# A graph network layer on one core: block 1's positions and five derived matrices at other places of the start

## The chip, the core and the metric

The kernel runs on one core of one Trainium2 chip. The core has TensorE (PE in the profile; its weight loads are PEld), VectorE (DVE), ScalarE (ACT), GpSimd (POOL) and SyncE (SP), each with a queue of its own that it works off in program order. The metric is the device time of one execution in microseconds; lower is better.

## The reference

128 graphs of 64 nodes with 128 channels; `adj` is 0 or 1, symmetric, with about one edge in eight. For every edge a message is computed by a three-layer network from the two nodes' rows, summed at the receiving node, and a second three-layer network updates the nodes:

```python
def _mlp(x, w0, b0, g0, be0, w1, b1, g1, be1, w2, b2):
    h = relu(x @ w0 + b0)
    h = layernorm(h, g0, be0)
    h = relu(h @ w1 + b1)
    h = layernorm(h, g1, be1)
    return h @ w2 + b2

messages = _mlp(concat([f_i, f_j]), *msg) * coupling_matrix[..., None]
agg = sum(messages, axis=2)
updated = part_feats + _mlp(concat([part_feats, agg]), *upd)
```

All of it is float32. The eight message and update weights are 128x128 (the first layers 256x128).

## The kernel before, in words

**Tiles.** Only existing edges are computed. Two graphs make a pair p (64 pairs); each graph has 640 slots for its edges, five tiles of 128. A quad q is two pairs, 20 tiles, five chunks n of four tiles (512 edges), so there are 160 chunks. A block b is four pairs (16 blocks, ten chunks each).

**Edges to slots.** For a block, `rank` (VectorE, L359) scans the adjacency rows, `count` (TensorE) and `count_out` (ScalarE) give running totals, and `place` (GpSimd, L384 to L388) makes the tile `pos`, the slot of each edge. `place_out` (L397, two GpSimd instructions) multiplies it by the adjacency into `posall`, which has one half for even and one for odd blocks. For a pair, `distance` (ScalarE, L482) and `make_tp` (VectorE, L488) make a 0/1 matrix from slot to receiving node, `marks` (L513, TensorE) multiplies it with `posall`, and `compare` (L521, VectorE) gives the matrix of the sending nodes. Both are copied by DMA into the tile `s` (`stack`, L504).

**Layers.** `rows` (L453 and L455) multiplies a block half's nodes with the first layer's weights in the PSUM bank `mu`; `rows_hi` (ScalarE, L467, `abh`) and `rows_lo` (VectorE, L473, `abl`) take it out. `layer0` (L539) multiplies `s` with these rows into the one bank `hps`, and ScalarE takes it out with a relu as `h` (L542). `stats0` transposes `h` (L548) and takes the statistics (L552). `layer1` (L609) runs eight iterations behind, in the banks `z0` and `z1` in turn; its bias times each edge's standard deviation is put there first, either by ScalarE (`seed`, L597, six chunks in ten) or by a matmul (L606) with `sdT`, the turned deviations, and a table `b1t`. ScalarE takes it out as `y` (L612), `stats1` (L619) follows. `weights` (L682) and `reduce` (L695) sum over the edges of a node, and a `Unit` of each block applies the update network.

**Standard deviations.** Once per quad: `var0_of` (five small GpSimd instructions, L249 to L253), `root_of` (ScalarE `m_sd` L259, then `sh` on ScalarE L566 and GpSimd L567), `turn_root` (TensorE, L572) and `root_out` (ScalarE, `sdT`, L577).

**Derived matrices.** `derivation` makes 13 matrices of the weights once: a layer norm's gain and centring are folded into the next layer's weights (`centred`: ScalarE scales to `wg`, L177; a product with the matrix of means, L181; VectorE subtracts, L186), its shift into the next bias (`shift`: ScalarE broadcasts `beb`, L204; two products, L207 and L208; a ScalarE copy, L197), and some are products or transposes (`plain`, L212, L216, copy L197). The first eight, up to `c2u`, belong to the message network and to the link between both; the last five (`ub0b`, `u1c`, `bu1b`, `u2c`, `cu2b`) are needed by the units alone, the first of which starts at iteration 23. `bias_table` (iteration 3: ScalarE `b1hi` L647, then GpSimd L649 to L653) and `bias_part` (GpSimd, L659, iterations 4 to 8) make the table `b1t` from `b1b`.

**The order.** It is written out by hand. After a start section with the first three chunks of layer 0, a loop runs over iterations n; `at(n, place, fn, ...)` puts a piece of work into place "a", "m", "b", "k", "x", "x1", "x2", "e0", "e1" or "e" of an iteration:

```python
        for n in range(last + 1):
            run(n, "a")
            run(n, "m")
...
                layer1(n - L1)
            run(n, "b")
...
                layer0(n if n >= QC else n + LEAD)
...
                stats0(n - 1 if n > QC else n + 1)
            run(n, "k")
...
                stats1(n - L1)
            for k in ("x", "x1", "x2", "e0", "e1", "e"):
                run(n, k)
```

Here QC is 5, LEAD is 3 and L1 is 8. Iterations 0 and 1 hold chunks 3 and 4 of layer 0; iterations 2 to 4 hold none; from iteration 5 on, iteration n holds chunk n of layer 0, and from iteration 8 on, chunk n - 8 of layer 1. The queue of each engine holds its part of this order.

A derived matrix with place n has its ScalarE preparation at (n-1, "x"), its products at (n, "x") and what takes it out at (n+1, "m"). The 13 matrices have the places 1, 2, 4, 5, 6, 7, 9, 10, 11, 12, 14, 15, 16, and all use the one `mu` bank (`ubank`), as do `rows` (block 1: iterations 8 and 13) and the units. The `z` banks serve the start section's marks, and then layer 1 from iteration 8 on. For block 1, `place` is at (2, "e") and `place_out` at (4, "e"); the marks of its first pair (4) are at iterations 5 and 6. For later blocks `place_out` is seven iterations ahead of the block's first chunk.

After the loop a path for graphs that don't fit stands behind a flag and isn't taken.

Of the kernel before, what the change touches and what calls it, by code (L numbers as in the profile page):

```python
# [23 lines left out]
def tile_gnn(  # L24
# [50 lines left out]
    QC = QT // CH  # L75
# [91 lines left out]
    nball = const.tile([P, NB], F32, name="nball")  # L167
    W = {}

    def derivation(bank):  # L170


        def centred(w, g, name):

            def ahead():
                wg = W[name, "g"] = const.tile([P, C], F32, name="wg", bufs=2)
                nc.scalar.activation(wg, w, AF.Copy, scale=g)  # L177

            def product():
                ps = bank()  # L180
                nc.tensor.matmul(ps[:, :C], lhsT=mean_m, rhs=W[name, "g"], start=True, stop=True)  # L181
                return ps

            def empty(ps):
                W[name] = const.tile([P, C], F32, name=name)
                nc.vector.tensor_tensor(W[name], W.pop((name, "g")), ps[:, :C], op=ALU.subtract)  # L186
            return ahead, product, empty

        def plain(name, fn, ahead=lambda: None):
            def product():  # L190
                ps = bank()
                fn(ps[:, :C])
                return ps

            def empty(ps):
                W[name] = const.tile([P, C], F32, name=name)
                nc.scalar.copy(W[name], ps[:, :C])  # L197
            return ahead, product, empty

        def shift(w, be, bias, name):  # L200

            def ahead():
                beb = W[name, "b"] = const.tile([P, P], F32, name="beb", bufs=2)
                nc.scalar.copy(beb, be.to_broadcast([P, P]))  # L204

            def fn(ps):
                nc.tensor.matmul(ps, lhsT=W.pop((name, "b")), rhs=w, start=True, stop=False)  # L207
                nc.tensor.matmul(ps, lhsT=ones_row, rhs=bias, start=False, stop=True)  # L208
            return plain(name, fn, ahead)

        def product_of(l, r, name):
            return plain(name, lambda ps: nc.tensor.matmul(ps, lhsT=l(), rhs=r, start=True,  # L212
                                                           stop=True))

        def turned(w, name):
            return plain(name, lambda ps: nc.tensor.transpose(ps, W[w], ident))  # L216

        return [
            centred(w1, g0c, "w1c"),
            shift(w1, be0c, b1r, "b1b"),  # L220

            centred(w2, g1c, "w2c"),
            turned("w2c", "w2cT"),
            product_of(lambda: W["w2cT"], u0b, "w2u"),
            shift(w2, be1c, b2r, "c2b"),
            turned("c2b", "c2bT"),
            product_of(lambda: W["c2bT"], u0b, "c2u"),
            product_of(lambda: ones_row, ub[0], "ub0b"),
            centred(u1, ug[0], "u1c"),
            shift(u1, ube[0], ub[1], "bu1b"),  # L230
            centred(u2, ug[1], "u2c"),
            shift(u2, ube[1], ub[2], "cu2b"),
        ]
# [55 lines left out]
    def edge_path(es):  # L289
# [32 lines left out]
        def zbank(k):  # L322
            return ps_z[k].tile([P, CH * C], F32, name=f"z{k}")
# [4 lines left out]
        def at(n, place, fn, *args):  # L328
            plan.setdefault((n, place), []).append((fn, args))
# [482 lines left out]
        for b in range(NB):  # L812
            o = b * CPB
            if b > 1:
                at(max(o - 25, 0), "a", load_adj, b)
                at(max(o - 12, 0), "a", load_x, b)
            if b > 0:
                r = max(o - 12, 1)
                at(max(o - 14, 0), "m", rank, b)
                at(r, "x", count, b)  # L820
                at(r + 1, "a", count_out, b)
                at(r + 1, "a", degrees, b)
                at(max(o - 9, r + 1), "e", place, b)
                at(max(o - 7, r + 3), "e", place_out, b)
                at(max(o - 7, 13), "m", odd_weights, b)
                at(o - 3, "x", turn_x, b)
                at(o - 2, "a", turn_x_out, b)
            for half, n in ((0, o - 2), (1, o + 3)):
                if n >= 0:
                    at(n, "x2", rows, b, half)  # L830
                    at(n + 1, "a", rows_hi, b, half)
                    at(n + 1, "m", rows_lo, b, half)
        for b in reversed(range(NB)):
            o = b * CPB
            n = o + QC + SC
# [35 lines left out]
        for p in range(NP):  # L871
            n = p * TG * 2 // CH
# [18 lines left out]
        for q in range(NQ):  # L891
            n = q * QC + QC if q else LEAD
# [86 lines left out]
        def turn_x_out_rest():  # L979
            nc.scalar.copy(blocks[0]["xnT"][:, 2 * P:PB * P], blocks[0].pop("x_ps")[:, 2 * P:])  # L980

        for n, (ahead, product, empty) in zip([n for n in range(1, 20) if n % QC != 3],
                                       derivation(ubank)):
            def keep(n=n, product=product):
                W["ps", n] = product()
            at(n - 1, "x", ahead)
            at(n, "x", keep)
            at(n + 1, "m", lambda n=n, empty=empty: empty(W.pop(("ps", n))))
        at(3, "b", bias_table)
        for c in range(QC):  # L990
            at(4 + c, "e", bias_part, c)
# [55 lines left out]
    with ExitStack() as es:  # L1047
        es.enter_context(tc.manual_schedule())
        flag = edge_path(es)
# [160 lines left out]
```

## Time and profile before

| | us |
|---|---|
| median of 4 runs | 577.57 |
| lowest and highest of them | 575.86, 577.91 |
| the profiled execution | 576.62 |
| its span, first to last instruction | 574.9 |
| TensorE busy | 549.0 |
| VectorE busy | 479.5 |
| ScalarE busy | 476.8 |
| GpSimd busy | 339.4 |

Lines of the profile name the engine, the source line, the operation, and what it writes from what it reads. In a timeline the first two numbers are start and duration in us, and the bracket at the end says how long the engine stood idle before and what released it. A timeline joins neighbouring instructions of one kind. Where instructions of one engine follow each other without a gap, the step from one start to the next is what one costs; the durations overlap a little. Of a matmul the end is modelled. Windows give, for a stretch, its length and the busy time of PE, PEld, DVE, ACT and POOL (with the number of instructions), then the granted TensorE clock (1.00 is full), the DMA engines' busy share and GB/s.

### The profile page before, as it was taken

How to read it: one execution, taken by the hardware profiler on the slowest of the kernel's cores; microseconds unless marked ns; L12 is line 12 of the kernel's file. 1: busy time of each engine (PE TensorE's matmuls, PEld its weight loads, DVE VectorE, ACT ScalarE, POOL GpSimd, SP SyncE). 2: the span in 40 equal slices, each digit the busy share in tenths (PEclk: the TensorE clock that was granted, in tenths of full speed). 3: DMA queues.
4: the chain of work that ended last, by engine and by line, in shares of the span. 5: the costliest groups of instructions: out<-in, count | busy, mean ns of one | idle time of the engine just before them, and what ended most of it. 6: DMA issues, size and time to landing. Idle time of an engine off the chain costs nothing. (4 is left out here: it accounts for less than half of the span.)

```text
span 574.9 us, 15748 instructions
## 1 busy us (share of the span) xinstructions
PE 549.0 (95%) x5303; PEld 514.9 (90%) x5303; DVE 479.5 (83%) x1944; ACT 476.8 (83%) x1149; POOL 339.4 (59%) x898
## 2 busy tenths in 40 slices
PE   6798999999999999999999999999999999998894
PEld 4587889999999999999999999999999999988883
DVE  5668789797989889798989979798988979896686
ACT  6677979898888989898888989888898989886434
POOL 3344465665757666565767656575766656556342
PEclk8889999999999999999999999999999999999998
DMA  4464536465554555468553654555376564631201
GB/s 101 102 144 106 130 94 141 94 115 130 125 133 106 140 110 130 105 110 153 111 143 83 139 115 116 127 125 133 93 144 116 123 107 100 135 93 33 34 21 40
DMA packets 90769, 63.21 MB, mean 110 GB/s; under 512 B 57398, under 2 KB 74812, under 8 KB 90684
## 3 DMA queue, kind: packets, MB, share of 16 engines
q1 hardware_dynamic: 90396, 62.03, 49.1%
q8 instruction: 43, 0.70, 0.5%
q14 instruction: 42, 0.34, 0.2%
q10 hardware_dynamic: 288, 0.13, 0.1%
HBM read 6.82 MB, written 4.19 MB: 19 GB/s over the span
## 5 line engine op out<-in xcount | busy, mean ns | idle before, releaser
L552 DVE BATCH_NORM_STATS2 st<-hT 128x6 f32<-128x128 f32 x640 | 141.9, 284 | 36.7 <-PE hT L548 35.2
L609 PE MATMUL z<-w1c,h 128*128 128x128 f32 x1280 | 172.2, 277 | 0.0
L609 PEld LDWEIGHTS z<-w1c,h 128*128 128x128 f32 x1280 | 161.0, 192 | 8.3 <-issue 5.1
L597 ACT ACTIVATE z<-b1b,m_sd 128x128 f32<-128x128 f32 x360 | 133.6, 371 | 8.7
L619 DVE BATCH_NORM_STATS2 st<-y 128x6 f32<-128x128 f32 x640 | 137.5, 276 | 2.7 <-ACT y L612 1.4
L612 ACT ACTIVATE y<-z 128x512 f32<-128x512 f32 x160 | 94.5, 591 | 26.7 <-PE z L609 24.9
L542 ACT ACTIVATE h<-hps,b0c 128x512 f32<-128x512 f32 x160 | 109.4, 684 | 3.8 <-PE hps L539 3.7
L548 PE MATMUL hT<-ident,h 128*128 128x128 f32 x640 | 98.2, 276 | 1.6 <-DVE st L552 1.5
L682 POOL TENSOR_TENSOR w<-oh,m_q 128x320 f32<-128x320 f16 x126 | 91.9, 741 | 9.9 <-PE hT L548 5.3
L539 PE MATMUL hps<-s,abl 128*128 128x512 f32 (+3 forms) x256 | 93.4, 376 | 1.7 <-DVE abl L473 0.9
L548 PEld LDWEIGHTS hT<-ident,h 128*128 128x128 f32 x640 | 76.8, 142 | 11.9 <-ACT h L542 1.3
L497 POOL CAST i<-tp 128x640 fp32r<-128x640 f16 x58 | 41.6, 717 | 66.7 <-DVE tp L488 48.7
L539 PE MATMUL hps<-s,abh 128*128 128x512 f32 (+3 forms) x256 | 79.5, 329 | 0.0
L695 PE MATMUL ys<-y,w 128*64 128x128 f32 x1280 | 76.9, 275 | 0.0
L695 PEld LDWEIGHTS ys<-y,w 128*64 128x64 f32 x1280 | 69.2, 137 | 4.2 <-issue 3.6
L249 POOL TENSOR_TENSOR m_d<-st 128x20 f32<-128x20 f32 x62 | 16.3, 263 | 91.0 <-DVE st L552 78.0
L521 DVE TENSOR_TENSOR j<-mk,cmpt 128x320 fp32r<-128x320 f32 x124 | 58.6, 472 | 3.1 <-PE mk L513 3.1
L539 PEld LDWEIGHTS hps<-s,abl 128*128 128x128 f32 x256 | 50.2, 196 | 3.6 <-ACT h L542 2.1
L482 ACT ACTIVATE d<-slot,mid 128x640 f16<-128x640 f16 x64 | 52.7, 824 | 0.0
L539 PEld LDWEIGHTS hps<-s,abh 128*128 128x128 f32 x256 | 50.5, 197 | 0.0
L473 DVE TENSOR_TENSOR abl<-mu,abh 128x512 fp32r<-128x512 f32 (+1 forms) x33 | 22.3, 675 | 31.3 <-ACT abh L467 31.1
L513 PE MATMUL mk<-tp,posall 128*128 128x320 f16 x126 | 38.3, 304 | 3.5 <-POOL posall L397 2.5
(224 smaller groups left out, 977.3 us busy)
## 6 DMA issues: line engine op xcount, KB each, us to landing
s<-i SPq DMA_DIRECT2D x124, 160.0 KB, 2.7
s<-j SPq DMA_DIRECT2D x124, 160.0 KB, 2.6
xn<-in_x_dram SPq DMA_DIRECT2D x15, 256.0 KB, 3.8
out_dram<-uo SPq DMA_DIRECT2D x15, 256.0 KB, 2.4
an<-in_adj_dram SPq DMA_DIRECT2D x16, 128.0 KB, 2.7
oh<-tp SPq DMA_TRANSPOSE x64, 3.4
xn<-in_x_dram SPq DMA_DIRECT2D x2, 128.0 KB
out_dram<-uo SPq DMA_DIRECT2D x2, 128.0 KB, 2.6
```

The lines of the kernel that those rows point to most:

```text
L482: nc.scalar.activation(D[p], slot, AF.Abs, bias=blocks[b]["mid"][:, q:q + 1], scale=-1.0)
L521: nc.vector.tensor_tensor(JR[p][:, c], MK.pop((p, k))[:, 0:HC], cmpt[:, c], op=ALU.is_equal)
L539: nc.tensor.matmul(ps[:, c:c + w], lhsT=ab[:, g % 4, :], rhs=s, start=(k == 0), stop=(k == 1))
L542: nc.scalar.activation(H[n], ps, AF.Relu, bias=b0c)
L548: nc.tensor.transpose(ps[:, t, :], H[n][:, t * P:(t + 1) * P], ident)
L552: nc.vector.bn_stats(ST0[q][:, CH * c + t, :], ps[:, t, :])
L597: nc.scalar.activation(Z[n][:, t, :], W["b1b"], AF.Copy, scale=SR[q][:, k:k + 1])
L609: nc.tensor.matmul(ps[:, t, :], lhsT=h[:, t * P:(t + 1) * P], rhs=W["w1c"], start=False, stop=True, skip_group_check=True)
L612: nc.scalar.activation(Y[n], ps, AF.Relu)
L619: nc.vector.bn_stats(ST1[q][:, CH * c + t, :], Y[n][:, t, :])
L682: (nc.vector if p == NP - 2 else nc.gpsimd).tensor_tensor(WT[p][:, :, g, :], OH[p][:, :, g * N:(g + 1) * N], Q[q][:, k:k + TG].unsqueeze(2 ...
L695: nc.tensor.matmul(YS[b][g * N:(g + 1) * N, k, :], lhsT=w[:, t, g, :], rhs=y, start=(t == 0), stop=(t == TG - 1))
```

## The change

Two things are moved; no operation is added or removed. `place_out` of block 1 goes from (4, "e") to (3, "a"). The last five derived matrices go from the places 11, 12, 14, 15 and 16 to 2, 3, 4, 5 and 6, and use the banks `z0` and `z1` (place n takes `z` of n % 2) instead of `mu`. At one place the steps of the first eight come first. `product` is now given its bank.

```diff
-    def derivation(bank):
+    def derivation():
...
-            def product():
-                ps = bank()
+            def product(ps):
                 nc.tensor.matmul(ps[:, :C], lhsT=mean_m, rhs=W[name, "g"], start=True, stop=True)
-                return ps
...
-                at(max(o - 7, r + 3), "e", place_out, b)
+                at(*((r + 2, "a") if b == 1 else (o - 7, "e")), place_out, b)
...
-        for n, (ahead, product, empty) in zip([n for n in range(1, 20) if n % QC != 3],
-                                       derivation(ubank)):
-            def keep(n=n, product=product):
-                W["ps", n] = product()
+        steps = derivation()
+        for n, k, bank in ([(n, k, ubank) for k, n in enumerate((1, 2, 4, 5, 6, 7, 9, 10))] +
+                           [(n, 6 + n, lambda n=n: zbank(n % 2)) for n in range(2, 7)]):
+            ahead, product, empty = steps[k]
+
+            def keep(n=n, k=k, bank=bank, product=product):
+                W["ps", k] = bank()
+                product(W["ps", k])
             at(n - 1, "x", ahead)
             at(n, "x", keep)
-            at(n + 1, "m", lambda n=n, empty=empty: empty(W.pop(("ps", n))))
+            at(n + 1, "m", lambda k=k, empty=empty: empty(W.pop(("ps", k))))
```

For block 1, r is 1 and o is 10; for b above 1, `o - 7` is what the maximum gave before.

More of the change, by code (lines that the diff above doesn't have):

```diff
@@ L189, in plain, with product @@
         def plain(name, fn, ahead=lambda: None):
-            def product():
-                ps = bank()
+            def product(ps):
                 fn(ps[:, :C])
-                return ps
             def empty(ps):
```

## The prediction

> **What bounds the kernel now.** I read the page first, then the waits of TensorE between 20 and 70 us, then the engines' timelines there, then windows cut where the granted clock changes.
>
> ```profile
> span 574.9 us, 15748 instructions
> PE 549.0 (95%) x5303; PEld 514.9 (90%) x5303; DVE 479.5 (83%) x1944; ACT 476.8 (83%) x1149; POOL 339.4 (59%) x898
> ...
> PEclk8889999999999999999999999999999999999998
> ```
>
> TensorE (PE) is the bound: busy 95%. What the change touches lies in the first 65 us, where PE has gaps. Its waits there (us in total, times, longest):
>
> ```profile
> PE mk L513 <- POOL posall L397: 2.5, 1, 2.5
> PE ma L572 <- POOL sh L567: 2.0, 2, 1.2
> PE mu L181 <- DVE abl L473: 1.4, 1, 1.4
> PE mu L453 <- DVE u1c L186: 1.3, 1, 1.3
> ```
>
> The first and the last have to do with the change: block 1's positions late by 2.5 us, and the u1c subtraction holding the one mu bank for 1.3 us ahead of `rows`. But a wait that goes is worth only the distance to the next one. For the first I read ScalarE's (ACT) timeline:
>
> ```profile
> 22.38 0.27 ACT L197 COPY b1b<-mu 128x128 f32<-128x128 f32 x1 [0.47 <-PE mu L208]
> 22.68 0.30 ACT L647 CAST b1hi<-b1b 128x128 fp32r<-128x128 f32 x1
> ...
> 26.73 0.31 ACT L259 ACTIVATE m_sd<-m,eps_c 128x20 f32<-128x20 f32 x1 [1.79 <-POOL m L253]
> 27.07 0.22 ACT L566 CAST sh<-m_sd 128x40 fp32r<-128x40 f32 x1
> 27.20 0.72 ACT L495 CAST i<-tp 128x640 fp32r<-128x640 f16 x1
> 27.82 0.82 ACT L482 ACTIVATE d<-slot,mid 128x640 f16<-128x640 f16 x1
> 28.56 0.67 ACT L542 ACTIVATE h<-hps,b0c 128x512 f32<-128x512 f32 x1
> ```
>
> The last row empties the only hps bank, and ends at 29.23. PE's next layer 0 (chunk 6) needs that bank and started at 29.47. So nearly all of the 2.5 us wait lies beside a second one: ACT works in program order, and this eviction stands behind a root that waits for GpSimd (POOL), which ran `bias_table` and `var0_of(0)` from 23.06 to 26.70, started by b1hi.
>
> **GpSimd's part.** `place_out(1)` moves from behind the `sh` subtraction (27.59, 1.52 us) to iteration 3's start. POOL ends `pos` at 21.61 and was idle until b1lo at 23.06, so the 1.52 us fit into 1.45 us of hole; b1lo would be 0.07 late, less than the 0.30 below. It is moved past no DMA. If the marks of pair 3 (22.98) had to wait for the same tile, they lose about 0.15 us, which the ACT chain covers; bounds 0 and 0.15, I take 0. Behind it, `bias_part` ends some 1.3 us earlier than at 34.68; no one waits for it.
>
> **What the five steps add to iterations 2 to 7.** Slots (start to start) from the same operations later in the trace: ub0b 0.41 on PE, bu1b and cu2b 0.32 + 0.41 = 0.73 each (55.81 to 56.54), u1c and u2c 0.14 each (48.95 to 49.09): 2.15 us. ACT: three copies of about 0.20, two weight scalings of 0.29, two broadcasts of 0.19: 1.56 us. VectorE: two subtractions of 0.20. Their vectors were issued by 12.3 us, ahead of need at 21; the z banks are free until iteration 8. No DMA is added.
>
> On PE, ub0b, u1c and bu1b push layer 0 of chunk 5 from 25.96 to about 26.95 and the marks of pair 4 to 27.65. That is hidden: both end before the ACT eviction. The cost is on ACT. The ub0b copy stands between b1b and b1hi: its product ends at about 22.75, so b1hi starts at 22.98, 0.30 late, and POOL's chain and m_sd with it. Behind m_sd come the u2 scaling (0.29) and the bu1b copy (0.20), ahead of the eviction: 28.56 + 0.30 + 0.29 + 0.20 = 29.35. It ends at 30.02, so chunk 6's layer 0 starts at 30.05 instead of 29.47, 0.58 late.
>
> From there PE is solid until layer 1 of chunk 0 (34.75 before), and its clock decides:
>
> ```profile
> 5.32:8.73 3.41, 1.77 (x19) 1.02 (x18) 2.85 (x6) 2.81 (x6) 2.67 (x7) 1.00 0.46 111
> ...
> 12.14:15.56 3.42, 2.56 (x9) 1.75 (x9) 1.74 (x5) 2.65 (x5) 0.00 (x0) 0.50 0.21 39
> ...
> 22.38:25.80 3.42, 1.90 (x22) 1.43 (x22) 2.55 (x9) 1.45 (x4) 2.56 (x7) 1.00 0.80 199
> 25.80:29.21 3.41, 0.91 (x5) 0.48 (x6) 0.45 (x2) 2.45 (x5) 2.40 (x7) 1.00 0.60 141
> 29.21:32.62 3.41, 3.41 (x15) 3.14 (x16) 2.98 (x8) 1.94 (x6) 3.41 (x3) 0.50 0.36 87
> ```
>
> The second column is PE's busy time, the third from the end the granted clock. It changes on a grid of 3.41 us. A stretch with PE busy 0.91 us (27%) was followed by a closed clock (0.50), one with 1.77 (52%) too; one with 1.90 (56%) was not. In the closed stretch chunk 6's layer 0 to chunk 7's took 29.47 to 32.30 = 2.83 us; at full clock the same slots are 0.67 (43.78 to 44.45) + 0.44 (44.45 to 44.89) + 0.14 (marks) + 0.15 (62.43 to 62.58) + 0.14 (42.52 to 42.66) = 1.54. So closed time loses 1 - 1.54/2.83 = 46%, 1.56 us per stretch.
>
> In the changed kernel PE has work from 26.05 to about 28.1, 2.05 us or 60% of the stretch 25.80 to 29.21 on this grid: it keeps the clock, narrowly. Then layer 0 of chunk 7 starts at 30.05 + 1.54 + 0.73 (cu2b) = 32.32, against 32.30, and takes 0.56 (47.81 to 48.37) where it took 0.71: **fill -0.1 us**. With one closed stretch it is -0.1 + 1.56 = +1.5.
>
> The Trainium skill ("TensorE: Matmul & The Clock Gate", "HAM oscillation") gives the rule as no PE gaps above about 3.4 us; the trace differs, since a gap of 2.5 us sufficed. By that rule the clock would hold here whatever the order, and only the -0.1 would stand; the row decides. The same page (Part 1) calls the window free-running and not reset at a kernel's start: then the grid falls elsewhere in each run. One trace can't show that; it speaks against counting on the clock.
>
> **What leaves iterations 11 to 17.** ub0b: the next matmul needs sdT, which ACT ended at 46.64, and started at 46.66: 0.06, not 0.41. u1c: 0.14.
>
> ```profile
> 52.89 0.32 PE L453 MATMUL mu<-w0a,xnT 128*64 128x128 f32 x1 [1.31 <-DVE u1c L186]
> ```
>
> Without the subtraction `rows` starts 1.3 + 0.2 us earlier. But ACT is solid from 48.09 to 54.72; only the 0.19 broadcast and the 0.06 go there, so abh starts at 53.90 and the y eviction of chunk 6 at 54.38 (55.10 before), the h eviction of chunk 14 ends at 55.55, and layer 0 of chunk 15, which needs its bank, runs at 55.6 (57.46): 1.86. VectorE, solid as well, starts the statistics of chunk 14 at 57.25 (58.64): 1.39. POOL, root and `turn_root(2)` follow: 61.04 (62.43). Next on PE, cu2b's 0.73 is gone: layer 1 of chunk 9 at 61.19 (63.30), 2.11. ACT, behind the root, reaches y of chunk 9 at 62.67 (64.50): 1.83. Both engines are nearly solid from there, and both must be earlier for the rest: bounds 1.39 (the root chain) and 2.11 (PE); I take **1.85**, ACT's, which is last.
>
> **Sum.** -1.85 - 0.1 = -1.95 us. The profiled execution took 576.62 around its span of 574.9; that gives 574.67. It lies 0.95 below the median of 577.57, inside the runs' 575.86 to 577.91, so I carry the difference to the median: 575.6.
>
> **Rivals.** (B) The clock closes once in the fill: -1.85 + 1.5 = -0.4, 577.2. For it: 60% is near the 56% and 52% on either side, and on a grid shifted by 1 us (26.8 to 30.2) PE's work is only 1.45 us, 43%. Against: the grid of this trace; and a shifted grid can also cost the kernel before more. (D) The 2.5 us wait is gained outright: if the eviction of chunk 5 doesn't hold PE, chunk 6 starts at 28.1, 1.95 earlier than I put it: 573.7. For it: the wait is the longest of its window; against: one hps bank and ACT's order. (C) Slower: the clock stays closed from 30 us for three stretches, as the trace shows from 8.73 to 18.97, when stretches 78% and 75% busy didn't open it. Price 10.24 x 0.46 = 4.7, net +2.8, 580.4. It decides from 1.95 / 0.46 = 4.2 us of closed clock. Against: behind 29.21 PE was 100% busy and the clock opened after one stretch. (E) The five steps' place doesn't matter, their cost is only moved, and iteration 13's wait returns behind ACT: no change, 577.6.
>
> **Numbers.** Forecast 0.45, B 0.30, D 0.10, C 0.07, E 0.08. 0.3% of the median is 1.73 us, about what a measurement can tell from no change. The forecast with its bounds (-1.5 to -2.2) lies past it two times in three, 0.30; B one time in five, 0.06; D always, 0.10: faster 0.46. Slower: C, and 0.01 of E: 0.08. The rest is 0.46. The range leaves out C and D: above, B and E with 0.3 us; below, the forecast's bound of 2.2 and one more microsecond, for runs of before that lose a second half stretch of clock where the new order doesn't: 574.4 to 577.9.
>
> **What the profile after should show.** No posall wait on PE; posall at about 21.6 on POOL; the eviction of chunk 5 at about 29.3, and PE idle some 2 us ahead of 30.05; a clock of 1.00 from 29 to 33; layer 1 of chunk 0 near 34.7; no u1c wait; `turn_root(2)` near 61.0; layer 1 of chunk 9 near 61.2. Wrong if that layer 1 is later than 62.5 with the clock open, or if layer 0 of chunk 6 starts before 29.

## The result, and the profile after

| | before | after |
|---|---|---|
| median, us | 577.48 (78 runs) | 575.57 (52 runs) |
| lowest, highest | 575.86, 580.64 | 573.43, 581.13 |
| ratio of the times, 95% interval | | 0.9971 (0.9962 to 0.998) |
| profiled execution, its span | 576.62, 574.9 | 576.14, 574.4 |

The median is 1.91 us lower, 0.33%; the ratio says 0.29%. Single runs spread over 5 us and 8 us. In the profiled executions the spans differ by only 0.5 us, and why that is so is most of this study.

The page after, in the lines shown of before:

```profile
span 574.4 us, 15753 instructions
PE 550.6 (96%) x5303; PEld 515.6 (90%) x5303; DVE 479.7 (84%) x1944; ACT 476.8 (83%) x1149; POOL 340.1 (59%) x898
...
PEclk9999999999999999999999999999999999998999
```

The clock of the first slices isn't 1.00 in truth: this trace's first clock record is the opening near 19 us, and the matmuls of 7 to 19 us have the durations of a closed one. What the record shows is a dip in the 37th slice, which before hasn't.

TensorE's (PE) waits from 20 to 70 us, as before (us in total, times, longest). Source lines after are 1 to 4 smaller than before:

```profile
PE ma L568 <- POOL sh L563: 2.3, 2, 1.5
PE hps L535 <- ACT h L538: 2.0, 2, 1.6
PE mu L180 <- DVE abl L469: 1.4, 1, 1.4
PE hT L544 <- DVE st L548: 0.4, 1, 0.4
```

The waits on posall and u1c are gone. In the place of the first stands one on the h eviction of ScalarE (ACT), 1.6 us, where the forecast had some 2 us. PE's timeline shows it at the first layer 0 piece of chunk 6, and further down the two places named in the prediction:

```profile
30.55 0.33 PE L535 MATMUL hps<-s,abl 128*128 128x128 f32 x1 [1.59 <-ACT h L538]
...
60.79 0.31 PE L568 MATMUL ma<-ident,sh 128*80 128x128 f32 x1 [1.47 <-POOL sh L563]
60.93 1.06 PE L605 MATMUL z<-w1c,h 128*128 128x128 f32 x8
```

They were forecast at 30.05, 61.04 and 61.19.

**Chunk by chunk.** The y eviction of a chunk by ACT is a good milestone: it comes once per iteration, and between closed clock stretches it repeats to 0.04 us from kernel to kernel. Its start after minus its start before, us, with the h eviction of chunk 3 ahead of it, which lies before anything that changed:

| | h 3 | y 0 | y 3 | y 4 | y 6 | y 7 | y 9 | y 12 | y 147 | y 149 | y 158 |
|---|---|---|---|---|---|---|---|---|---|---|---|
| after - before | +0.62 | +0.44 | +0.44 | -0.17 | -0.82 | -1.48 | -2.07 | -2.09 | -2.11 | -0.49 | -0.49 |

It has four parts. This execution began 0.62 us late, in work that is the same. The fill (iterations 2 to 7) is 0.18 us shorter. Between chunks 3 and 12 the changed kernel gains 2.53 us, and keeps them to 0.02 us over 135 chunks. Then it loses 1.62 us at chunks 148 and 149. Windows cut at the clock's changes show that last loss, after first (length; busy time of PE, PEld, DVE, ACT, POOL; clock, DMA share, GB/s):

```profile
26.33:29.74 3.41, 2.43 (x12) 1.57 (x12) 2.16 (x6) 2.16 (x6) 2.56 (x8) 1.00 0.76 180
...
514.43:517.84 3.41, 1.50 (x13) 1.42 (x13) 1.56 (x8) 2.36 (x6) 1.79 (x6) 1.00 0.00 0
517.84:521.25 3.41, 3.41 (x17) 3.31 (x16) 0.72 (x4) 2.59 (x7) 1.58 (x3) 0.50 0.00 0
```

The windows of before on its own grid:

```profile
513.90:517.31 3.41, 2.66 (x22) 2.28 (x20) 2.95 (x15) 3.00 (x8) 0.18 (x1) 1.00 0.41 97
517.31:520.72 3.41, 2.25 (x18) 2.19 (x19) 0.79 (x4) 1.98 (x5) 1.60 (x6) 1.00 0.03 5
```

In both kernels PE stands idle for 1.91 us there, ahead of the turn of block 12's `uy`. After, all of that idle time falls into one stretch of the clock's grid (PE 44% busy), and the next stretch is closed. Before, the same idle time is cut by a grid line (78% and 66%), and the clock stays open. In the fill it is the other way round: after, 71% busy and open; before, 27% and closed. Of the traces without unread matmuls at that place, all five with moved matrices close there (after, e2_matrices, e3_ub0b, e4_u1c_stays, e7_late_copies), and the two without (before, e1_positions) don't. Whether the change helps to bring that about or the grids fell so by chance, seven traces don't show.

### The profile page after: what moved, and what is told of

It is laid out like the page before. It is cut to its first block, busy times and chain, and to the rows that moved or that the text cites. A ratio compares the mean times of both kernels' runs of the same rounds, so it can differ in the third digit from the quotient of the medians.

```text
span 574.4 us, 15753 instructions
## 1 busy us (share of the span) xinstructions
PE 550.6 (96%) x5303; PEld 515.6 (90%) x5303; DVE 479.7 (84%) x1944; ACT 476.8 (83%) x1149; POOL 340.1 (59%) x898
## 5 line engine op out<-in xcount | busy, mean ns | idle before, releaser
L463 ACT CAST abh<-mu 128x512 fp32r<-128x512 f32 (+1 forms) x33 | 18.9, 573 | 23.9 <-PE mu L451 23.9
```

## The experiments

Theory: the gain is 2.5 us of the work taken out of iterations 11 to 17; the posall wait alone is worth nothing, since ACT's eviction of chunk 5 covers it; and TensorE's clock, by where its grid falls, adds or takes up to 3 us in a single run. Rivals: the wait is gained outright; the gain is the clock's in the fill. Times are medians beside runs of before on the same chip (577.55 for the first four, 577.62 for the next four, 577.72 for the last two). "Chunk n" means the y eviction against before's.

**e1_positions: `place_out` alone.**

```diff
-                at(max(o - 7, r + 3), "e", place_out, b)
+                at(*((r + 2, "a") if b == 1 else (o - 7, "e")), place_out, b)
```

> Block 1's positions at iteration 3, derived matrices where they were. Theory (the ScalarE eviction of chunk 5 covers the wait): the 2.5 us wait on posall is gone from TensorE's list and returns as a wait of 2 us or more on that eviction; chunk 6's layer 0 starts at most 0.2 us earlier against chunk 5's end than before; every later y eviction is within 0.3 us of before's, once the start's own offset is taken off; time within 0.5 us of before. Rival (the wait is gained outright): chunk 6's layer 0 1.4 us or more earlier, time 576.2 or less.

577.79, ratio 1.001 (0.9991 to 1.0028). PE's waits from 20 to 70 us:

```profile
PE hps L539 <- ACT h L542: 2.6, 1, 2.6
PE ma L572 <- POOL sh L567: 2.0, 2, 1.2
```

The 2.5 us on posall have become 2.6 us on the h eviction. Chunk 0 is at +0.52 with chunk 3's h eviction at +0.54, and every chunk from there to the last stays at +0.49 to +0.52: nothing gained or lost. The rival that the wait is gained outright has fallen. As before, the clock was closed behind the fill in this trace (29.70 to 33.11); the positions alone with an open clock weren't run.

**e2_matrices: the five matrices alone** (the diff's last part, with `place_out` as before).

> The five matrices moved, positions at iteration 4 as before. Theory: the same 2.5 us are saved between the y evictions of chunks 3 and 9 as with the whole change; in the fill chunk 6's layer 0 starts within 0.2 us of where the whole change has it, since the eviction covers posall; TensorE is busy 0.4 us less between 26 and 29 us (marks, transpose and u2 product come behind posall), so the clock closes there on more of the grids: time between the changed kernel's 575.6 and 577.2. Rival (most of the gain is the posall wait): 577.0 or more, and chunk 6's layer 0 over 0.5 us later than with the whole change.

577.6, ratio 1.0007 (0.9995 to 1.002): outside the theory's range and inside the rival's. The trace tells which of the two was right. Chunks 3 to 9 gain 2.52 us (+1.68 to -0.84), as with the whole change. PE does wait for posall:

```profile
PE mk L509 <- POOL posall L393: 1.4, 1, 1.4
```

but chunk 6's layer 0 starts at 30.34, against 30.55 with the whole change: the wait costs nothing by itself. The loss comes after it. PE was busy 1.97 us in the clock's stretch from 26.60 to 30.01, and the next was closed:

```profile
26.60:30.01 3.41, 1.97 (x10) 1.29 (x11) 0.70 (x3) 2.65 (x7) 2.40 (x7) 1.00 0.58 142
```

Chunk 0 is 1.24 us later than with the whole change on its open grid, though chunk 6's layer 0 began 0.21 earlier: 1.45 us. The profile also has a closed stretch at 519 us, and loses another 1.6 us there. So the earlier positions seem to matter through the clock; the last run, e10_matrices_busy, tests that.

**e3_ub0b: only ub0b moved, and the positions.**

```diff
+                           [(2, 8, lambda: zbank(0))] +
+                           [(n, k, ubank) for k, n in ((9, 12), (10, 14), (11, 15), (12, 16))]):
```

> Only ub0b of the five is moved; positions moved. Theory now (chunk 4 of layer 1 needs the deviations of quad 0, turned long before, so ub0b's slot lay on TensorE's path): between the y evictions of chunks 3 and 4 some 0.55 to 0.65 us are saved, and they are kept to chunk 12. The prediction's step (the next matmul waits for sdT): 0.06 us there.

577.24, ratio 1.0003 (0.9987 to 1.0019). Chunk 3 is at +1.02, chunk 4 at +0.41, chunk 12 at +0.40: 0.61 us saved, and kept. The prediction's 0.06 was wrong. This execution's fill lay in a closed stretch twice as long (6.83 us).

**e4_u1c_stays: all moved but u1c.**

```diff
+                           [(n, 6 + n, lambda n=n: zbank(n % 2)) for n in (2, 4, 5, 6)] +
+                           [(12, 9, ubank)]):
```

> Four of the five matrices and the positions moved; u1c stays at iteration 12 in the mu bank, so the wait of rows on its subtraction stays. Theory (that wait lies beside a solid ScalarE): between the y evictions of chunks 3 and 9 some 2.0 to 2.2 us are saved, 0.3 to 0.5 less than with the whole change. Rival (the wait of 1.3 us counts in full): 1.0 to 1.2 us.

576.98, ratio 1.0011 (0.9987 to 1.0035; the runs spread from 576.02 to 581.38). Chunk 3 is at -0.35, chunk 9 at -2.23: 1.88 us saved, 0.63 less than with the whole change (2.51). PE still waits 1.3 us for u1c. So that wait and u1c's slot, 1.45 us together, are worth 0.63: more than the 0.3 to 0.5 that I expected, and less than half of the 1.45 that the rival counts.

**e5_busy: the changed kernel, with unread matmuls in three of PE's idle stretches.**

```diff
+        def busy(k, bank=None):
+            t = bank() if bank else ps_y.tile([P, PB, C], F32, name="ys").rearrange("p q c -> p (q c)")
+            for _ in range(k):
+                nc.tensor.matmul(t[:, 0:P], lhsT=mean_m, rhs=mean_m, start=True, stop=True)
...
+                if b == NB - 4:
+                    at(n + t[10], "x", busy, 8, ubank)
                 at(n + t[10], "x", turn, u, "uy")
...
+        at(3, "x2", busy, 6)
+        at(5, "x2", busy, 7)
```

> The changed kernel with matmuls whose product no one reads in three of TensorE's idle stretches: 6 behind rows in iteration 3, 7 behind the u2 product in iteration 5, and 8 ahead of the turn of block 12's uy near 514 us. Theory (the difference between runs of one kernel is where the clock closes on its grid): no closed stretch between 20 and 550 us in the profile; the y evictions keep the changed kernel's offsets of 2.1 us within 0.3 us to the last chunk; median 0.7 to 1.5 us under the changed kernel's 575.6. Rival (the clock has nothing to do with the 1.6 us that the changed kernel's profile lost at 517 us): the loss stays, median as the changed kernel's or above it.

574.42, ratio 0.9938 (0.9921 to 0.9955). PE's timeline at the idle place of 514 us:

```profile
514.12 0.60 PE L742 MATMUL ma<-ident,ysum 128*128 128x128 f32 x4
514.55 1.95 PE L325 MATMUL mu<-mean_m 128*128 128x128 f32 x16
516.63 0.66 PE L742 MATMUL ma<-ident,uy 128*128 128x128 f32 x4
```

The turn of `uy` runs as it did, the clock stays open, and the offset holds to the last chunk (-1.84 at chunk 12, at 149 and at 158). The 1.6 us were the clock's. All three numbers of the theory held.

**e6_busy_start: and three times three unread matmuls in the start section**, ahead of `marks_here(0)`, `layer0(0)` and `layer0(2)`, as `busy(3)`.

> As the run before, and 3 more unread matmuls ahead of each of three waits of the start section (marks of pair 0, layer 0 of chunk 0, layer 0 of chunk 2). Theory: TensorE's clock is not closed, or for one stretch less, between 5 and 19 us; chunk 3's y eviction comes 0.5 to 2 us earlier. Rival (the start is bound by the chain of ScalarE and VectorE, not by the clock): chunk 3's y eviction moves by less than 0.3 us, or later by up to 0.5 us where the matmuls delay the work behind them.

572.0, ratio 0.9903 (0.9885 to 0.992). The trace has no closed stretch from its first clock record at 5.1 us to 564.9 us, and chunk 3 comes 2.19 us earlier than before, 2.9 us earlier than in the run above. So in that run the start had lost these 2.9 us to the clock, more than the 0.5 to 2 that I expected.

**e7_late_copies: ACT's steps out of the way of chunk 5's eviction** (place n, step, bank, preparation, copy):

```diff
+                [(2, 9, lambda: zbank(1), 1, 3), (4, 11, lambda: zbank(1), 3, 5),
+                 (5, 10, lambda: zbank(0), 3, 6), (5, 8, lambda: zbank(1), 4, 6),
+                 (6, 12, lambda: zbank(0), 5, 7)]):
```

> The changed kernel with the five matrices' ScalarE steps out of the way of chunk 5's eviction: u1c at iteration 2 (prepared in 1), u2c at 4 (prepared in 3), bu1b and ub0b at 5 (copied in 6, bu1b prepared in 3), cu2b at 6. Theory (0.79 us stand ahead of that eviction: the ub0b copy through b1hi, the u2 scaling, the bu1b copy): the eviction starts 0.6 to 0.8 us earlier against the start of chunk 4's, chunk 6's layer 0 and everything behind it too, with the clock open. Rival (TensorE's own work in iterations 4 and 5 takes its place, since ub0b and bu1b now stand behind the marks of pair 4): gain under 0.2 us.

575.35, ratio 0.9968 (0.9953 to 0.9983): no better than the change within the noise. From the b1b copy to the eviction are 6.18 us before (22.38 to 28.56), 6.85 with the change (22.97 to 29.82) and 6.52 here (22.39 to 28.91): half of the 0.67 is won back, not all. What took its place is on GpSimd (POOL):

```profile
21.82 1.50 POOL L393 TENSOR_TENSOR posall<-pos,an 64x256 f16<-64x256 f32 x2
23.41 0.46 POOL L645 TENSOR_TENSOR b1lo<-b1b,b1hi 128x128 f32<-128x128 f32 x1
```

b1hi was ready at 22.99, as before, but b1lo now stands behind `place_out` and starts at 23.41 (23.06 before). The 1.5 us don't quite fit into the hole of 1.45, the more so as the u1 scaling, now in iteration 1, makes `pos` 0.13 later. In e1_positions the same distance is 6.38: `place_out` alone costs 0.20, not the 0.07 of the prediction. The theory's number missed. By the measure that the expectation named, the start of chunk 4's eviction, the gain is 0.16 us (9.77 to 9.61), inside the rival's range; but the rival's cause, PE's own work, isn't what took its place: chunk 6's layer 0 starts 0.71 us behind the start of chunk 5's eviction here, and 0.73 with the change.

**e8_late_busy: both.**

> Both together: the ScalarE steps out of the way as in the run before, and the unread matmuls of the start, the fill and near 514 us. If both theories hold: the gains of the two add, 573 to 574.5. If the unread matmuls delay the work behind them where the gaps are now shorter: 0.3 to 0.8 us above the better of the two.

571.96, ratio 0.9902 (0.9884 to 0.992): the same as e6_busy_start (572.0), and below the 573 to 574.5 expected, since e6_busy_start alone had gained more than I thought. With the clock open the copies' place is worth nothing that can be told apart; chunk 0 is at -2.25 against -2.19.

**e9_before_busy: the kernel before with the unread matmuls.** As in e6_busy_start, but in iteration 5 eleven ahead of the marks:

```diff
+        at(3, "x2", busy, 6)
+        at(5, "k", busy, 11)
```

> The kernel before with the unread matmuls of the run with the busy start: 3 ahead of each of three waits of the start section, 6 behind rows in iteration 3, 11 ahead of the marks of pair 4 in iteration 5 (where it waits for posall), 8 ahead of the turn of block 12's uy. Theory (with the clock open throughout, the change is worth what iterations 11 to 17 give, 2.5 us, and the fill by itself little): no closed stretch up to 550 us; 2.4 to 3.0 us above the changed kernel with the same matmuls (572.0), so 574.4 to 575.0. Rival (most of the change's gain is the clock behind 29 us): within 1.2 us of 572.0.

575.7, ratio 0.9967 (0.9953 to 0.9982). The clock stays open from the start. Against e6_busy_start: chunk 0 0.21 us earlier (0.07 of it already at chunk 3's h eviction, so the change's fill costs 0.14 to 0.21 when the clock is open in both), chunk 12 2.33 later, chunk 158 2.34 later. That is the change's worth without the clock, in these two traces. The median differs by 3.7, more than the theory's 2.4 to 3.0: the nine runs fall into 574.24 to 574.62 (three) and 575.43 to 576.02 (six), with the same recorded mean clock of 0.995 to 0.996. The profiled one is of the lower group. What makes the upper group isn't settled, so 2.34 is shown for the lower group alone. The rival, within 1.2 us of 572.0, has fallen.

**e10_matrices_busy: the matrices alone, with the unread matmuls** (`busy, 6` at (5, "k")).

> The five matrices moved, positions at iteration 4 as before, with the unread matmuls: as in the run before, but 6 ahead of the marks of pair 4. Theory (the earlier positions are worth something only because TensorE has work between 26 and 29 us and the clock stays open): with the clock open anyway, chunk 0's y eviction is within 0.4 us of the changed kernel's with unread matmuls, the time within 0.5 us of 572.0. Rival (the earlier positions are worth the 1.4 us that TensorE waits for posall when only the matrices are moved): 573.2 or more.

572.21, ratio 0.9917 (0.9901 to 0.9933): 0.2 us above e6_busy_start (572.0). Chunk 0 is 0.12 later and chunk 12 0.14. So with the clock open the earlier positions, beside the moved matrices, are worth under 0.2 us. The same edit is worth 2.0 with the clock left to the gaps (e2_matrices 577.6, the whole change 575.57), which points to the clock; the two profiled executions show 1.24 of it, and the rest isn't traced.

## Why the prediction was right

The time, the sign and the range held: 575.6 forecast, 575.57 measured, and the 1.91 us lie, as I put it, past 0.3% by little. Step by step:

**The wait on posall.** Right. It was replaced by the h eviction (1.59 us of wait, and 2.6 when alone), and the run with the positions alone gained nothing.

**The chain on ScalarE in the fill.** Right in kind. The eviction moved by 0.67 us against the b1b copy, where I had 0.79; chunk 6's layer 0 came at 30.55 - 0.62 = 29.93 on before's scale, where I had 30.05. ACT's timeline after:

```profile
22.97 0.27 ACT L193 COPY b1b<-mu 128x128 f32<-128x128 f32 x1 [0.25 <-PE mu L204]
23.19 0.27 ACT L193 COPY ub0b<-z 128x128 f32<-128x128 f32 x1
23.35 0.30 ACT L643 CAST b1hi<-b1b 128x128 fp32r<-128x128 f32 x1
...
27.55 0.31 ACT L255 ACTIVATE m_sd<-m,eps_c 128x20 f32<-128x20 f32 x1 [1.79 <-POOL m L249]
...
29.82 0.68 ACT L538 ACTIVATE h<-hps,b0c 128x512 f32<-128x512 f32 x1
```

Two terms were off and partly cancel. The ub0b copy delays b1hi by 0.08 us (0.38 behind the b1b copy, 0.30 before), not by 0.30. From b1hi to m_sd are 4.20 us, 4.05 before: `place_out` in front of b1lo costs 0.15 here and 0.20 alone, where I had 0.07 and let the ub0b copy hide it. The two steps behind m_sd cost 0.44, forecast 0.49.

**The fill's sum, -0.1 us.** Right on these two grids: -0.18. Layer 0 of chunk 7 came at 32.86 - 0.62 = 32.24 on before's scale, where I had 32.32. But the sum lets the closed stretch cost the kernel before 1.56 us, and that price doesn't hold there. With the clock open (e9_before_busy) the way from chunk 6's layer 0 to layer 1 of chunk 0 took 5.45 us (27.24 to 32.69), against 5.62 closed (29.47 to 35.09): only 0.17 less. A wait on VectorE that the prediction doesn't have came in the clock's place:

```profile
30.55 0.66 PE L554 MATMUL hT<-ident,h 128*128 128x128 f32 x4 [0.97 <-DVE st L558]
...
27.41 0.49 DVE L527 TENSOR_TENSOR j<-mk,cmpt 128x320 fp32r<-128x320 f32 x1 [3.01 <-PE mk L519]
...
29.61 0.88 DVE L558 BATCH_NORM_STATS2 st<-hT 128x6 f32<-128x128 f32 x4
```

VectorE had stood idle for 3.01 us until the marks of pair 4 (27.07), which came behind `posall` (done at 27.01), and then worked without a gap up to these statistics. With the positions early (e6_busy_start) the wait isn't there, and the same way took 4.97 us. So with the clock open in both, the change's fill costs 0.14 to 0.21 us, not the 1.3 that its terms (0.58 and 0.73) add up to.

**The clock in the fill.** Right on this execution's grid, which fell where I had assumed it to (71% busy, open). Of other runs I had said that the grid falls elsewhere; the spread of 8 us agrees, and e5_busy, e6_busy_start and e8_late_busy, which narrow it to 1.3 to 2.1 us (in six runs each). But I looked for closed stretches in the fill alone. The idle place at 514 us cost 1.6 us in each of the five traces where a stretch took all of it in; it hid three quarters of the gain in the profiled execution. The bound that I read from the rows, closed up to 52% busy and open from 56%, isn't one: in e2_matrices 58% (1.97 of 3.41) was followed by a closed stretch, and in e1_positions 55% (1.86) by an open one.

**Iterations 11 to 17, -1.85 us.** The size was off: 2.53. The term that failed is ub0b, 0.06 in the prediction and 0.61 in e3_ub0b. I had let the matmul behind it wait for the sdT that ACT ended at 46.64. PE's timeline before:

```profile
46.01 0.31 PE L572 MATMUL ma<-ident,sh 128*80 128x128 f32 x1 [0.83 <-POOL sh L567]
46.25 0.48 PE L212 MATMUL mu<-ub0r,ones_row 1*128 1x128 f32 x2
46.66 0.50 PE L606 MATMUL z<-b1t,sdT 80*128 80x512 f32 x1
```

and after:

```profile
46.45 0.31 PE L568 MATMUL ma<-ident,sh 128*80 128x128 f32 x1 [0.83 <-POOL sh L563]
46.51 0.48 PE L602 MATMUL z<-b1t,sdT 80*128 80x512 f32 x1
```

Now the matmul starts 0.06 after `turn_root(1)`, ahead of any sdT of that root: it belongs to chunk 4, which is still in quad 0, whose sdT had been there since iteration 7. The two names are alike and the times met by chance. So the whole step from the turn to that matmul went down from 0.65 to 0.06. Without that term the rest was near: 1.92 measured against 1.79, and u1c with its wait 0.63 of 1.45, since ACT was solid, as said.

**Why the number still fits.** By the trace the change is worth 2.53 + 0.18 = 2.7 us on these two grids, up to chunk 147, and 2.34 with the clock open in both; the lowest times of the two kernels differ by 2.43 (575.86 and 573.43), and the median moved 1.91. The forecast of 1.95 was 0.7 too small in its largest term. What took the rest from the median isn't shown; the loss at 514 us is a candidate. The forecast's case, the clock open in the fill, is what the profile shows; how many of the 52 runs it holds for can't be seen, since only their mean clocks are recorded. That the median came within 0.1 us of the forecast was luck.

**The rivals.** B (closes in the fill): seen in e2_matrices, at a price of 1.45 us against my 1.56. C (closed for three stretches behind 30 us): not seen in these traces; the longest there was 6.83 us, in e3_ub0b. D fell with e1_positions, E with the chunk table.

## What to carry to other kernels

A wait that goes is worth the distance to the next one: look for the in-order engine that frees the same bank, and read its queue up to there, as here for 2.5 us that were worth nothing. When a wait is put down to an operand by its name, check which generation of that operand the instruction reads; a release time that happens to fit is no proof. Where runs of one kernel differ by more than the edit under study, compare milestones inside the traces from one clock change to the next, and give TensorE unread work in its known idle places: here six such places cost 3.6 us (575.57 to 572.0), more than the change itself brought.

## What the runs showed of the hardware

TensorE's clock was closed for one or more stretches of 3.41 us after stretches in which PE was busy for 27%, 44%, 52% or 58%, with no idle time above 2.5 us, and stayed open after 55%, 56%, 66%, 71% and 78%. The shares overlap, so PE's modelled busy time alone doesn't set it. The time of its weight loads doesn't part these cases either: 1.42 us were followed by a closed stretch (after, 514.43 to 517.84), 1.38 us by an open one (e1_positions, 22.87 to 26.28). What does set it isn't settled by these runs. Three matmuls whose result no one reads, put ahead of each of three waits in the first 14 us, kept the clock open there and brought the first chunks 2.9 us forward.
